# A two-layer graph network on one core: q, k and v by seven half-size products, with x1 parked in DRAM and a new loop order

## The chip, the cores and the metric

The kernel runs on one core of a Trainium2 chip. The metric is the time of one execution in microseconds (us) on the device. The fast runs of each kernel told here lie within 0.36% of each other (3150.13 to 3161.24 us in split_gap, the widest). Each ratio to the kernel before is from runs on one chip. The experiments ran on three chips, on which the kernel before took 2766.76 to 2768.5 us, so times are also compared across them. "Round" means one pass of the kernel's loop: each of its stages works on one of the 128 batches, each stage on another one. SBUF and PSUM are the on-chip memories in which the kernel allocates its tiles; all its matmuls write to PSUM, in tiles of 512 columns, called "banks" here. The "granted clock" is the share of TensorE's full clock that the profile records (1.00 is full speed, 0.50 half).

## The reference, cut to what matters

```
x: (128, 128, 512) float32; adj: (128, 128) float32
# layer 0
h = relu(layernorm(x));  x = x + einsum('nm,bmd->bnd', adj, h) @ W0 + b0         # x1
# layer 1
h = relu(layernorm(x))
q, k, v = split(h @ Wqkv)            # Wqkv 512 x 1536, 8 heads of 64
a = softmax(where(adj == 0, -inf, q k^T / 8))
o = (a v) @ Wp + bp
out = x + o + layernorm(o) * gamma + beta
```

Everything is float32. A product of 512x512 by 512x512 (four batches of 128 rows) stands behind each of q, k and v; Strassen's form does it with seven products of 256x256 by 256x256 in place of eight.

## The kernel before

The parts that the change and the argument touch (cuts marked). Each engine's instructions start in the order in which the program emits them (`manual_schedule`): in this kernel's trace, rounds 7 to 115, TensorE's 8 blocks of a round, VectorE's 23 instructions, ScalarE's 8 and GpSimd's 7 came in that order in 107 of 107 rounds. They wait for each other's results: VectorE for pp, 686.6 us in all. The order of the loop's calls is therefore part of the kernel.

```python
    psum = ctx.enter_context(tc.tile_pool(name="psum", bufs=4, space=bass.MemoryType.PSUM))
    ctx.enter_context(tc.manual_schedule())
    ...
    def stats_of(src):                      # three VectorE steps, then GpSimd
        nc.vector.bn_stats(st, src)
        nc.vector.bn_aggr(mv, st)
        nc.vector.tensor_scalar(ve, mv[:, 1:2], EPS, None, op0=ALU.add)
        nc.gpsimd.tensor_tensor(rs, ve, minus_half, op=ALU.pow)
        return mv[:, 0:1], rs

    def relu_norm(dst, src, mean, rs):      # one VectorE step, then ScalarE
        nc.vector.tensor_scalar(shift, mean, rs, -1.0, op0=ALU.mult, op1=ALU.mult)
        nc.scalar.activation(dst, src, AF.Relu, bias=shift, scale=rs)
    ...
    def qk(i, k):                           # m = 0..7: q and k of a group of four
        for c in range(C):
            nc.tensor.matmul(p, lhsT=wqkv_sb[:, c, m * P:(m + 1) * P],
                             rhs=H1T[g][:, c, :, :].rearrange("p b n -> p (b n)"),
                             start=(c == 0), stop=(c == C - 1))
        nc.scalar.copy(QKT[g][:, m, :, :].rearrange("p b n -> p (b n)"), p)
    ...
    for i in range(2 - LOAD, B + 1):
        at(norm1_out, i + 8)
        ...
        at(scores, i)
        at(softmax_shift, i)
        at(qk, i + G, 0)
        at(flip_probs, i - 1)
        at(softmax_exp, i)
        at(norm0, i + 11)
        at(mix, i + 10)
        at(softmax_divide, i)
        at(norm0_out, i + 11)
        at(qk, i + G, 1)
        at(attend, i - 1)
        at(values, i + 4)
        at(flip, i + 8)
        at(project, i - 1)
        at(finish, i - 1)
        at(layer0, i + 9)
```

What the stages are: `scores` (matmuls ps, VectorE adds the mask), `softmax_shift` (maximum, difference), `softmax_exp` (ScalarE), `softmax_divide` (VectorE sums and reciprocal, GpSimd product sq, then an exchange through DRAM), `flip_probs` (VectorE transpose pT), `attend` (matmuls po, ScalarE copy oT), `project` (matmuls pp, VectorE add o and its statistics), `finish` (VectorE, GpSimd o+x1, VectorE, store). `norm0`, `norm0_out`, `mix` and `layer0` are layer 0; `norm1_out` and `flip` prepare h for q, k and v.

## Time and profile before

| | before |
|---|---|
| time, median of the runs beside the changed kernel | 2768.86 us |
| busy share: TensorE, VectorE, GpSimd, ScalarE | 97%, 59%, 36%, 24% |
| mean granted TensorE clock | 0.987 |
| mean length of a round (batches 7 to 115, from the starts of the oT copy) | 20.70 us |

In the lines below, a timeline row gives start and length in us, the engine, the source line, the operation, what it writes and reads, how many instructions were merged, and in brackets how long the engine had idled before it and what released it. Rows of a merged block end a little after the next block starts, because the ends of matmuls are modelled.

### The profile page before, as it was taken

How to read it: one execution, taken by the hardware profiler on the slowest of the kernel's cores; microseconds unless marked ns; L12 is line 12 of the kernel's file. 1: busy time of each engine (PE TensorE's matmuls, PEld its weight loads, DVE VectorE, ACT ScalarE, POOL GpSimd, SP SyncE). 2: the span in 40 equal slices, each digit the busy share in tenths (PEclk: the TensorE clock that was granted, in tenths of full speed). 3: DMA queues.
4: the chain of work that ended last, by engine and by line, in shares of the span. 5: the costliest groups of instructions: out<-in, count | busy, mean ns of one | idle time of the engine just before them, and what ended most of it. 6: DMA issues, size and time to landing. Idle time of an engine off the chain costs nothing. (4 is left out here: it accounts for less than half of the span.)

```text
span 2762.8 us, 29275 instructions
## 1 busy us (share of the span) xinstructions
PE 2666.9 (97%) x10241; PEld 1312.7 (48%) x10241; DVE 1632.5 (59%) x2951; ACT 666.1 (24%) x1026; POOL 987.8 (36%) x902
## 2 busy tenths in 40 slices
PE   6999999999999999999999999999999999999974
PEld 3444444444444444444444444444444444444432
DVE  3365665665665665665665665665665665665544
ACT  2222222222222222222222222222222222222110
POOL 3233333333333333333333333333333333333222
PEclk9999999999999999999999999999999999999986
DMA  4233333333333333333333333333333333332221
GB/s 165 64 97 105 100 102 104 100 101 104 102 101 103 103 100 103 103 99 103 103 101 103 102 102 102 102 103 100 103 103 103 99 103 104 99 103 96 76 77 61
DMA packets 223636, 276.76 MB, mean 100 GB/s; under 512 B 24704, under 2 KB 155904, under 8 KB 223488
## 3 DMA queue, kind: packets, MB, share of 16 engines
q1 hardware_dynamic: 223488, 274.89, 30.8%
q8 instruction: 80, 1.31, 0.2%
q14 instruction: 68, 0.56, 0.1%
HBM read 140.57 MB, written 134.22 MB: 99 GB/s over the span
## 5 line engine op out<-in xcount | busy, mean ns | idle before, releaser
L194 PE MATMUL pqk<-h1T,wqkv_sb 128*128 128x512 f32 x2048 | 934.5, 600 | 5.7 <-issue 5.7
L127 POOL TENSOR_TENSOR rs<-ve,minus_half 128x1 f32<-128x1 f32 x384 | 266.4, 694 | 1425.8 <-DVE ve L125 1425.8
L142 ACT ACTIVATE h<-x,shift,rs 128x512 f32<-128x512 f32 x256 | 208.3, 814 | 1537.7 <-DVE shift L141 1537.7
L194 PEld LDWEIGHTS pqk<-h1T,wqkv_sb 128*128 128x128 f32 x2048 | 370.3, 190 | 393.8 <-issue 378.8
L263 DVE TENSOR_TENSOR o<-pp,bp_b 128x512 f32<-128x512 f32 x128 | 88.4, 691 | 686.6 <-PE pp L261 686.6
L261 PE MATMUL pp<-wp_sb,oT 128*128 128x512 f32 x1024 | 470.2, 603 | 3.4 <-ACT oT L255 3.4
L203 PE MATMUL pv<-wqkv_sb,h1T 128*128 128x512 f32 x1024 | 473.2, 605 | 0.0
L165 PE MATMUL pl<-w_sb,yT 128*128 128x512 f32 x1024 | 465.5, 598 | 0.0
L261 PEld LDWEIGHTS pp<-wp_sb,oT 128*128 128x128 f32 x1024 | 197.4, 193 | 254.0 <-issue 209.7
L165 PEld LDWEIGHTS pl<-w_sb,yT 128*128 128x128 f32 x1024 | 196.5, 192 | 245.6 <-issue 245.6
L237 POOL TENSOR_TENSOR sq<-s,sm 128x1024 f32<-128x1024 f32 x128 | 244.3, 1908 | 177.9 <-DMA x<-in_x_dram 98.4
L203 PEld LDWEIGHTS pv<-wqkv_sb,h1T 128*128 128x128 f32 x1024 | 184.5, 190 | 207.1 <-issue 207.1
L229 ACT ACTIVATE s<-s 128x1024 f32<-128x1024 f32 x128 | 135.3, 1057 | 364.3 <-DVE s L226 364.3
L273 DVE SCALAR_TENSOR_TENSOR t<-t,rs,o 128x512 f32<-128x512 f32 x128 | 96.2, 751 | 214.1 <-POOL o L272 214.1
L177 POOL TENSOR_TENSOR x<-x,beta_b 128x512 f32<-128x512 f32 x128 | 162.2, 1267 | 152.1 <-ACT h L142 149.3
L252 PE MATMUL po<-pT,v 128*64 128x128 f32 x2048 | 144.5, 285 | 57.0 <-DVE pT L244 50.7
L252 PEld LDWEIGHTS po<-pT,v 128*64 128x64 f32 x2048 | 113.1, 140 | 160.1 <-DVE pT L244 104.1
L121 DVE BATCH_NORM_STATS2 st<-x 128x6 f32<-128x512 f32 x256 | 172.5, 674 | 5.6 <-DMA x<-in_x_dram 1.1
L156 PEld LDWEIGHTS pmix<-adjT,h 128*128 128x128 f32 x1024 | 136.8, 195 | 78.5 <-issue 58.8
L215 PEld LDWEIGHTS ps<-qkT 64*128 64x128 f32 x2048 | 124.2, 187 | 97.1 <-issue 97.1
L151 POOL TENSOR_TENSOR x<-x,b_b 128x512 f32<-128x512 f32 x128 | 161.8, 1264 | 15.0 <-ACT h L142 15.0
L220 DVE TENSOR_TENSOR s<-ps,maskb 128x512 f32<-128x512 f32 x256 | 163.5, 680 | 0.0
(36 smaller groups left out, 2011.1 us busy)
## 6 DMA issues: line engine op xcount, KB each, us to landing
d<-sq SPq DMA_DIRECT2D x128, 512.0 KB, 2.6
sx<-d SPq DMA_DIRECT2D x512, 128.0 KB, 2.9
x<-in_x_dram SPq DMA_DIRECT2D x128, 256.0 KB, 2.7
d<-h SPq DMA_DIRECT2D x128, 256.0 KB, 2.0
h1x<-d SPq DMA_DIRECT2D x512, 64.0 KB, 2.0
out_dram<-t SPq DMA_DIRECT2D x128, 256.0 KB, 2.1
wqkv_sb<-in_L_gnn_w_qkv_dram SPq DMA_DIRECT2D x1, 3072.0 KB, 16.6
w_sb<-in_L_gnn_weight_dram SPq DMA_DIRECT2D x1, 1024.0 KB, 9.2
```

Of the source, the lines that this page charges most:

```text
L121: nc.vector.bn_stats(st, src)
L127: nc.gpsimd.tensor_tensor(rs, ve, minus_half, op=ALU.pow)
L142: nc.scalar.activation(dst, src, AF.Relu, bias=shift, scale=rs)
L151: nc.gpsimd.tensor_tensor(X[i], X[i], b0_b, op=ALU.add)
L165: nc.tensor.matmul(p, lhsT=YT[i][:, c, :], rhs=w0_sb[:, c, :], start=(c == 0), stop=(c == C - 1))
L177: nc.gpsimd.tensor_tensor(X1[i], X1[i], beta_b, op=ALU.add)
L194: nc.tensor.matmul(p, lhsT=wqkv_sb[:, c, m * P:(m + 1) * P], rhs=H1T[g][:, c, :, :].rearrange("p b n -> p (b n)"), start=(c == 0), stop=(c ...
L203: nc.tensor.matmul(p, lhsT=H1T[g][:, c, j, :], rhs=wqkv_sb[:, c, 2 * D:], start=(c == 0), stop=(c == C - 1))
L220: nc.vector.tensor_tensor(s[:, e * C:(e + 1) * C, :], ps[e], m4, op=ALU.add)
L237: nc.gpsimd.tensor_tensor(sq, s.rearrange("p h (q r) -> p q h r", q=Q), sm.unsqueeze(1).unsqueeze(3).to_broadcast([P, Q, H, R]), op=ALU.mult)
L252: nc.tensor.matmul(p[e * HD:(e + 1) * HD, c, :], lhsT=V[i][:, h:h + HD], rhs=PT[i][:, e * C + c, :], start=True, stop=True)
L261: nc.tensor.matmul(p, lhsT=OT[i][:, c, :], rhs=wp_sb[:, c, :], start=(c == 0), stop=(c == C - 1))
```

## The change

The intent is to cut TensorE's work, which fills 97% of the span. For each of q, k and v of a group of four batches, seven products with half the rows, half the columns and half the depth are formed instead of eight. GpSimd forms the four sums of the left factor, VectorE the sums of the weights once at the start. The products are summed partly in the PSUM banks and partly by VectorE adds when a bank is read. To make room in SBUF, x1 is stored in DRAM and loaded again when it is needed; to make room in PSUM, the other matmuls get two banks in place of four. The loop is ordered anew as well.

```diff
-    psum = ctx.enter_context(tc.tile_pool(name="psum", bufs=4, space=bass.MemoryType.PSUM))
+    psum = ctx.enter_context(tc.tile_pool(name="psum", bufs=2, space=bass.MemoryType.PSUM))
 ...
+    def left_factors(g):
 ...
+        nc.gpsimd.tensor_tensor(s1, a21, a22, op=ALU.add)
+        nc.gpsimd.tensor_tensor(s2, s1, a11, op=ALU.subtract)
+        nc.gpsimd.tensor_tensor(s4, a12, s2, op=ALU.subtract)
+        nc.gpsimd.tensor_tensor(s3, a11, a21, op=ALU.subtract)
+        LEFT[g] = (a11, s1, s2, s4, s3, a12, a22)
+    def product(g, kind, k, p):             # four matmuls of 256 columns
 ...
+    def chain(g):                           # 3 x 7 steps, one per "yield"
 ...
+            product(g, kind, 0, X_);  nc.scalar.copy(r1, X_);  yield
+            product(g, kind, 1, Y_);  nc.scalar.copy(r5, Y_);  yield
+            product(g, kind, 2, X_);  nc.scalar.copy(r2, X_);  yield
+            product(g, kind, 3, Y_);  nc.vector.tensor_tensor(c12, Y_, r2, op=ALU.add);  yield
+            product(g, kind, 4, X_);  nc.vector.tensor_tensor(c22, X_, r5, op=ALU.add);  yield
+            product(g, kind, 5, Z_);  nc.vector.tensor_tensor(c11, Z_, r1, op=ALU.add);  yield
+            product(g, kind, 6, X_);  nc.scalar.copy(c21, X_);  yield
 ...
+        X1D[i] = dram.tile([P, D], F32, name="x1d", bufs=14)
+        nc.sync.dma_start(out=X1D[i], in_=X1.pop(i))
 ...   (the loop)
         at(scores, i)
+        at(reload, i - 1)
+        next(step, None)
         at(softmax_shift, i)
-        at(qk, i + G, 0)
+        at(flip, i + 7)
+        at(layer0, i + 8)
+        at(softmax_exp, i)
+        next(step, None)
         at(flip_probs, i - 1)
-        at(softmax_exp, i)
-        at(norm0, i + 11)
-        at(mix, i + 10)
         at(softmax_divide, i)
-        at(norm0_out, i + 11)
-        at(qk, i + G, 1)
+        at(norm1_out, i + 8)
+        at(norm0, i + 10)
+        at(mix, i + 9)
+        next(step, None)
+        at(norm0_out, i + 10)
         at(attend, i - 1)
-        at(values, i + 4)
-        at(flip, i + 8)
+        next(step, None)
+        if j == G - 1 and 0 <= g + 2 < B // G:
+            left_factors(g + 2)
         at(project, i - 1)
         at(finish, i - 1)
-        at(layer0, i + 9)
+        next(step, None)
+        if j == G - 1:
+            next(step, None)
```

(The steps of `chain` are set on one line each here, and their allocations are left out.)

## The prediction

> **What bounds the kernel now.** I read the page's busy shares first, then the timeline of TensorE over a few rounds in the middle, then the timelines of the other engines over the same round.
>
> ```profile
> PE 2666.9 (97%) x10241; PEld 1312.7 (48%) x10241; DVE 1632.5 (59%) x2951; ACT 666.1 (24%) x1026; POOL 987.8 (36%) x902
> ```
>
> TensorE is busy for 97% of the span, no other engine for more than 59%. One round of the loop (one batch in each stage) on TensorE; columns are start us, length us, engine, line, operation, operands, count:
>
> ```profile
> 1403.04 1.05 PE L156 MATMUL pmix<-adjT,h 128*128 128x128 f32 x8
> 1403.93 3.60 PE L194 MATMUL pqk<-h1T,wqkv_sb 128*128 128x512 f32 x8
> ...
> 1408.60 3.70 PE L203 MATMUL pv<-wqkv_sb,h1T 128*128 128x512 f32 x8
> 1412.14 3.60 PE L261 MATMUL pp<-wp_sb,oT 128*128 128x512 f32 x8
> ...
> 1419.10 1.16 PE L215 MATMUL ps<-qkT 64*128 64x128 f32 x16
> ...
> 1423.73 1.05 PE L156 MATMUL pmix<-adjT,h 128*128 128x128 f32 x8
> ```
>
> The round repeats after 20.69 us (1403.04 to 1423.73) and the blocks follow each other with 0.0 to 0.2 us between. pp to pl starts 3.43 us apart (1412.14 to 1415.57 in the same view), so one 512-column instruction, of which there are two per matmul of the program, takes 0.429 us. Eight 128-column ones take 0.89 us, 0.111 each. So TensorE bounds it. But the other engines are in order, and the next three views (same round) show how little slack stands behind that. VectorE:
>
> ```profile
> 1402.58 1.28 DVE L220 TENSOR_TENSOR s<-ps,maskb 128x512 f32<-128x512 f32 x2
> ...
> 1408.42 1.21 DVE L234 TENSOR_REDUCE sm<-s 128x8 f32<-128x1024 f32 x1
> 1409.66 0.20 DVE L235 RECIPROCAL sm<-sm 128x8 f32<-128x8 f32 x1
> 1409.78 0.16 DVE L141 TENSOR_SCALAR shift<-mv,rs 128x1 f32<-128x1 f32 x1
> ...
> 1415.77 0.69 DVE L263 TENSOR_TENSOR o<-pp,bp_b 128x512 f32<-128x512 f32 x1 [5.21 <-PE pp L261]
> ...
> 1419.93 0.75 DVE L273 SCALAR_TENSOR_TENSOR t<-t,rs,o 128x512 f32<-128x512 f32 x1 [1.68 <-POOL o L272]
> ```
>
> GpSimd:
>
> ```profile
> 1403.59 1.27 POOL L177 TENSOR_TENSOR x<-x,beta_b 128x512 f32<-128x512 f32 x1 [1.18 <-ACT h L142]
> 1408.64 0.55 POOL L127 TENSOR_TENSOR rs<-ve,minus_half 128x1 f32<-128x1 f32 x1 [3.79 <-DVE ve L125]
> 1410.10 1.91 POOL L237 TENSOR_TENSOR sq<-s,sm 128x1024 f32<-128x1024 f32 x1 [0.91 <-DMA x<-in_x_dram]
> 1411.96 1.27 POOL L151 TENSOR_TENSOR x<-x,b_b 128x512 f32<-128x512 f32 x1
> ...
> 1418.63 1.26 POOL L272 TENSOR_TENSOR o<-o,x 128x512 f32<-128x512 f32 x1
> ```
>
> ScalarE:
>
> ```profile
> 1409.98 0.81 ACT L142 ACTIVATE h<-x,shift,rs 128x512 f32<-128x512 f32 x1 [1.99 <-DVE shift L141]
> ...
> 1411.16 0.59 ACT L255 COPY oT<-po 128x512 f32<-128x512 f32 x1
> ```
>
> Read them as one ring. VectorE adds the mask (1402.58), takes maximum, difference, sums and reciprocal (to 1409.86), gives ScalarE its shift (1409.78); ScalarE does the relu (1409.98) and then copies oT (1411.16 to 11.75); pp starts at 1412.14; VectorE waits for it (1415.77), finishes the output at 1420.68, adds x1, and begins the next mask at 1423.27. That ring has only tenths of slack: in the waits of this trace the weight load of pp stood for ACT's oT 120 times, 43.3 us in all, 0.36 each. What keeps it short is one detail of POOL: the rs of norm0 (1408.64) is made *before* the 1.91 us sq (1410.10), so the shift finds it ready.
>
> [...]
>
> ```profile
> 37.24 1.16 PE L156 MATMUL pmix<-adjT,h 128*128 128x128 f32 x8 [2.58 <-ACT h L142]
> ...
> 47.05 2.08 PE L156 MATMUL pmix<-adjT,h 128*128 128x128 f32 x8 [5.21 <-ACT h L142]
> ```
>
> After 2.58 us idle eight mix matmuls ran in 1.16 us, after 5.21 us in 2.08, and the pl block that followed took 5.53 instead of 3.60.
>
> **The change on TensorE.** Per group of four batches q, k and v took 48 matmuls = 96 instructions x 0.429 = 41.2 us. Strassen's form has 3 x 7 products x 4 matmuls of 256 columns = 168 instructions x 0.216 = 36.3 us. Weight loads (0.19 us each) stay hidden, since the mix blocks have one every 0.111. Saved: 4.9 us a group, 1.23 us a round, about 158 us in 128 rounds. Against it: 21 blocks a group instead of 12, each waiting for a read of its bank; blocks that wait for another engine now begin 0.1 to 0.2 us late. Estimate 0.3 to 0.6 us a round. TensorE alone would need about 20.0 us a round: 2,670 us in all, 3% less.
>
> **Other work.** ScalarE keeps its 12 copies a group. VectorE gets 9 adds of 128x512 out of PSUM a group (0.69 each as L220 and L263), 1.6 us a round on 12.5: 14 of 20, not full. POOL gets four adds a group, 4 x 1.27 = 5.1 us, 1.3 a round on 7.5. x1's trip is 0.5 MB a round, some 25 GB/s on the page's 100, with the reload a round ahead of its use: hidden. The eight weight sums are some 8 us once.
>
> **The order is what decides.** The diff also moves things in the loop. flip and layer0's add and stats now stand *before* flip_probs on VectorE, inside the ring (they were after the shift, in the idle time, and after the output). And POOL now gets, in this order, sq, x1+beta, rs of norm0; norm0's shift on VectorE waits for that rs, ScalarE's relu for the shift, the oT copy stands behind the relu, project behind oT. Walk the new ring with starts from the trace, each to the start of the next (us):
> - mask adds 1.31, maximum 1.25, difference 1.22, flip 0.70 (its row's mean), x1 add 0.72, stats 0.73 + 0.22 + 0.07, pT 1.17, sums 1.24, reciprocal until sq starts 0.44: 9.07
> - POOL sq 1.86, x1+beta 1.25, rs until the shift 0.58: 3.69
> - shift to relu 0.20, relu to oT copy 0.72, oT to pp 0.98: 1.90
> - pp to o add 3.63, add 0.72, stats 0.73 + 0.22 + 0.23, POOL rs 0.96, o+x1 1.30, last step to the next VectorE work 0.67: 8.46
>
> Sum 23.12 us. By the steps' places in the rounds, five of the nine adds of a group fall inside the ring (the first two steps and the one after finish; the others fall while VectorE waits for POOL or TensorE): 5 x 0.72 / 4 = 0.90. Ring: 24.0 us, against 20.0 for TensorE. **The ring becomes the bound**, and TensorE stands some 4 us before project in each round (its work up to the products before project ends about 11 us after the output, project starts at about 15). By the early trace such a gap is at the edge of costing clock: a throttled project is 1.2 to 2 us longer. I add 0.3 us a round on average: 24.3. POOL's four adds in every fourth round (from about 6.3 to 11.4 us after sq starts) end as project's rs is wanted, so cost about nothing.
>
> **The sum.** The first scores started at 120 us (weight loads begin early; one round later plus 8 us of weight sums, less TensorE work: same). About 120 full rounds: 120 x 24.3 = 2,916. The last nine rounds without layer 0 took 161 us and have the same order: 161. 120 + 2,916 + 161 = 3,197; I say 3,190.
>
> **Rivals.** (1) TensorE stays the bound: 2,600 to 2,680. It needs the ring below 20 us, that is VectorE not waiting for norm0's rs behind sq and beta, or shorter POOL work. The 97% and the clean cadence of before speak for it; the program order read from the diff, and that every engine of before ran in program order, against. Even with only busy times in the ring (no latencies) I get 22 + 0.9 us. (2) The clock falls in every round: project at half speed adds up to 3.4 us, 27 us a round, some 3,550. Gaps of 3.8 us in the early trace were throttled only for a part (mix 1.64 us, pl 4.84), so unlikely as a rule. (3) The queue of SyncE, which now also waits for the x1 store, delays flip or flip_probs: h1x would land some 7 us before its flip, sx more; no effect. (4) PSUM: two mm banks and one of cy and cz. Each bank's reader stands one or two blocks ahead; the waits fall in TensorE's new idle time.
>
> **Range and chances.** The uncertain terms are the clock (0 to 1.2 us a round) and the ring (23.0 to 24.5): 23.0 gives 3,040 and 25.2 gives 3,310. Should I have misread the order, the time falls to rival 1, or to a tie if only part of the ring opens: 6% faster, 4% within 2%, 90% slower.
>
> **What will show it.** Right: a round near 24 us; pp preceded by a TensorE idle of about 4 us released by ACT's oT; VectorE waiting 1.5 to 2.5 us at the shift of norm0 for POOL's rs; rs directly after the x1+beta add; TensorE busy near 80%; instructions of the products 0.216 us apart, 1.73 us a block of eight. Wrong: rounds below 21 us with TensorE above 95% (order misread), or a granted clock below 0.9 (rival 2), or waits at the products' banks or DMAs leading the list of waits.

## The result, and the profile after

| | before | after |
|---|---|---|
| time, median | 2768.86 us | 3312.85 us (3311.79 to 3313.65, 4 runs) |
| TensorE busy | 2666.9 us, 97% | 2774.4 us, 84% |
| mean granted clock | 0.987 | 0.906 |
| mean round | 20.70 us | 25.44 us |

The changed kernel is slower by 19.7%: ratio 1.1968, 95% interval 1.1948 to 1.1989. A ratio here is the mean time of one kernel's fast runs over that of the other's of the same rounds, so it is not quite the ratio of the medians quoted. The results are correct.

The page of the kernel after: busy times, and the row of the granted clock over 40 slices (tenths of full speed):

```profile
PE 2774.4 (84%) x12545; PEld 1829.2 (55%) x12545; DVE 1816.7 (55%) x3247; ACT 675.0 (20%) x1026; POOL 1140.8 (34%) x1030
...
PEclk9999989888989889898998988999988989889997
```

TensorE is no longer at its limit, and its busy time has grown although it does fewer columns: the clock row swings between 8 and 9 for the whole span, where before it stood at 9 until the end.

TensorE's timeline, the blocks around project (pp):

```profile
1621.55 1.99 PE L232 MATMUL cx<-h1T,wqk_sb 128*128 128x256 f32 x8
1627.30 3.70 PE L334 MATMUL pp<-wp_sb,oT 128*128 128x512 f32 x8 [3.75 <-ACT oT L328]
...
1650.00 5.10 PE L334 MATMUL pp<-wp_sb,oT 128*128 128x512 f32 x8 [3.53 <-ACT oT L328]
1654.93 1.89 PE L232 MATMUL cz<-wv_sb,h1T 128*128 128x256 f32 x8
...
1674.79 3.70 PE L334 MATMUL pp<-wp_sb,oT 128*128 128x512 f32 x8 [2.49 <-ACT oT L328]
```

In each round pp stands after an idle gap that ScalarE's oT copy ends: 2.5 to 4.0 us, 3.4 on average over rounds 7 to 115. The block at 1627.30 takes 3.5 us (the next one starts at 1630.84). The one at 1650.00 takes 4.9 us (to 1654.93), for the same eight instructions.

VectorE, GpSimd and ScalarE in the round before 1627.30:

```profile
1612.13 1.28 DVE L292 TENSOR_TENSOR s<-ps,maskb 128x512 f32<-128x512 f32 x2
...
1621.61 0.20 DVE L307 RECIPROCAL sm<-sm 128x8 f32<-128x8 f32 x1
...
1625.71 0.21 DVE L155 TENSOR_SCALAR shift<-mv,rs 128x1 f32<-128x1 f32 x1 [2.22 <-POOL rs L141]
1631.04 0.69 DVE L336 TENSOR_TENSOR o<-pp,bp_b 128x512 f32<-128x512 f32 x1 [5.11 <-PE pp L334]
```

```profile
1622.04 1.91 POOL L309 TENSOR_TENSOR sq<-s,sm 128x1024 f32<-128x1024 f32 x1 [2.63 <-DVE shift L155]
1623.91 1.26 POOL L191 TENSOR_TENSOR x<-x,beta_b 128x512 f32<-128x512 f32 x1
1625.13 0.55 POOL L141 TENSOR_TENSOR rs<-ve,minus_half 128x1 f32<-128x1 f32 x1
```

```profile
1625.96 0.81 ACT L156 ACTIVATE h<-x,shift,rs 128x512 f32<-128x512 f32 x1 [2.75 <-DVE shift L155]
1626.68 0.56 ACT L328 COPY oT<-po 128x512 f32<-128x512 f32 x1
```

This is the ring as the prediction read it from the diff. The reciprocal ends at 1621.81, sq follows on GpSimd, then x1+beta, then rs of norm0 (1625.13 to 1625.68); VectorE, idle for 2.22 us, makes the shift at 1625.71; ScalarE does relu and oT; pp starts at 1627.30; VectorE takes its output at 1631.04. From the view of waits:

```profile
PE pp L334 <- ACT oT L328: 400.4, 122, 4.0
...
DVE shift L155 <- POOL rs L141: 313.9, 135, 3.1
```

VectorE's wait for rs was 111.6 us in all before and is 313.9 now. TensorE's own wait for oT was 3.4 us before and is 400.4.

The same kernel in stretches of 1 us around the pp block at 1650.00 (after the busy times of TensorE, weight loads, VectorE, ScalarE and GpSimd come the granted clock, the DMA share and GB/s):

```profile
1648.00:1649.00 1.00, 0.00 (x0) 0.00 (x0) 0.58 (x2) 0.34 (x1) 0.38 (x1) 1.00 0.77 307
1649.00:1650.00 1.00, 0.00 (x0) 0.00 (x0) 0.23 (x1) 0.95 (x2) 0.44 (x1) 0.72 0.00 0
1650.00:1651.00 1.00, 1.00 (x1) 0.50 (x2) 0.00 (x0) 0.00 (x0) 1.00 (x2) 0.50 0.45 125
1651.00:1652.00 1.00, 1.00 (x3) 0.47 (x2) 0.00 (x0) 0.00 (x0) 1.00 (x1) 0.50 0.98 278
1652.00:1653.00 1.00, 1.00 (x3) 0.46 (x2) 0.00 (x0) 0.00 (x0) 0.92 (x2) 0.58 0.91 251
1653.00:1654.00 1.00, 1.00 (x3) 0.38 (x2) 0.00 (x0) 0.00 (x0) 0.92 (x2) 1.00 0.38 130
```

The clock halves some 3 us after TensorE went idle (at about 1646.5), stays at 0.50 for about 3.4 us and comes back at about 1652.8. Project, the block that ends the gap, has a granted clock of 0.50 for its first 2.8 us.

### The profile page after: what moved, and what is told of

The parts are those of the page before. It is cut to its first block, busy times and chain, and to the rows that moved or that the text cites. A ratio compares the mean times of both kernels' runs of the same rounds, so it can differ in the third digit from the quotient of the medians.

```text
span 3311.1 us, 34928 instructions
## 1 busy us (share of the span) xinstructions
PE 2774.4 (84%) x12545; PEld 1829.2 (55%) x12545; DVE 1816.7 (55%) x3247; ACT 675.0 (20%) x1026; POOL 1140.8 (34%) x1030
## 5 line engine op out<-in xcount | busy, mean ns | idle before, releaser
L334 PE MATMUL pp<-wp_sb,oT 128*128 128x512 f32 x1024 | 717.4, 866 | 400.4 <-ACT oT L328 400.4
L334 PEld LDWEIGHTS pp<-wp_sb,oT 128*128 128x128 f32 x1024 | 275.5, 282 | 779.6 <-ACT oT L328 449.4
L232 PE MATMUL cy<-sum,wqk_sb 128*128 128x256 f32 x1024 | 251.8, 389 | 2.4 <-POOL sum L214 2.4
L232 PE MATMUL cx<-h1T,wqk_sb 128*128 128x256 f32 x1024 | 250.1, 388 | 0.9 <-DVE qkT L269 0.9
L232 PE MATMUL cx<-sum,wqk_sb 128*128 128x256 f32 x1024 | 243.7, 381 | 6.5 <-issue 6.5
L232 PEld LDWEIGHTS cx<-sum,wqk_sb 128*128 128x128 f32 x1024 | 193.4, 191 | 72.2 <-issue 52.0
L155 DVE TENSOR_SCALAR shift<-mv,rs 128x1 f32<-128x1 f32 x256 | 48.5, 190 | 314.0 <-POOL rs L141 313.9
L232 PEld LDWEIGHTS cy<-sum,wqk_sb 128*128 128x128 f32 x1024 | 186.9, 190 | 52.0 <-issue 25.0
L232 PEld LDWEIGHTS cx<-h1T,wqk_sb 128*128 128x128 f32 x1024 | 188.2, 191 | 45.3 <-issue 13.0
```

The lines of the kernel that those rows point to most:

```text
L232: nc.tensor.matmul(p[:, half, :], lhsT=lhsT, rhs=rhs, start=first and half == 0 and c == 0, stop=k in (3, 5, 6) and c == 1, skip_group_che ...
L334: nc.tensor.matmul(p, lhsT=OT[i][:, c, :], rhs=wp_sb[:, c, :], start=(c == 0), stop=(c == C - 1))
```

## Experiments

Ten kernels were run, all correct, all in three timed rounds beside the kernel before. The **ring theory** says that the new order closed a loop of dependences longer than TensorE's work. The **clock theory** adds that TensorE's idle gap in each round lowers its clock. The rivals are that the products themselves cost TensorE more than their columns, that project is slow because of its bank or weights, and that x1's trip to DRAM delays something.

"Slow pp" below is a pp block longer than 4 us, counted over up to about 110 rounds in the middle of the profiled run (some rounds fall on a border of the views and are not counted). The time from oT's start to VectorE's add of o contains pp; it is 4.35 to 4.40 us with an undisturbed clock in all variants of the changed kernel whose project was not moved, so what is above 4.37 on average is put down to the clock.

| kernel | time us | ratio to before | mean round us | clock part of it us | slow pp |
|---|---|---|---|---|---|
| before | 2768.86 | 1 | 20.70 | 0 | 0 |
| after | 3312.85 | 1.197 | 25.44 | 2.0 | 85 of 93 |
| split_gap | 3156.53 | 1.140 | 23.84 | 0.4 | 24 of 99 |
| beta_late | 3033.97 | 1.096 | 23.04 | 0.8 | 53 of 103 |
| rs_first | 3033.28 | 1.096 | 23.04 | 0.9 | 56 of 103 |
| keep_busy | 3105.11 | 1.123 | 23.45 | 0 | 0 of 101 |
| order_alone | 3247.48 | 1.174 | 24.75 | 1.5 | 48 of 96 |
| order_alone_deep | 3144.52 | 1.136 | 23.89 | 1.2 | 68 of 100 |
| products_old_order | 2880.08 | 1.041 | 21.61 | 0 | 0 of 110 |
| x1_dram_alone | 2768.69 | 1.000 | 20.70 | 0 | not counted |
| open_ring_plain | 2732.24 | 0.988 | 20.57 | not in the ring | not counted |
| open_ring | 2572.36 | 0.929 | 19.34 | not in the ring | not counted |

### keep_busy: more work for TensorE in the gap

```diff
     def project(i):
         p = mm_psum("pp")
+        for c in range(3):
+            nc.tensor.matmul(p, lhsT=wp_sb[:, c, :P], rhs=wp_sb[:, c, :], start=True, stop=True)
         for c in range(C):
```

> The changed kernel with six extra matmul instructions (three calls of 128x512, 2.6 us) put into TensorE's idle time right before project, into project's own bank, which project then overwrites. Ring theory with the clock: TensorE gets 330 us more work and the kernel is faster, because the idle gap falls from 3.7 to about 1 us, project takes 3.4 us, the ring stays at 23.4: 3,050 to 3,090 us. Rival (project is slow because of its bank or its weights, or TensorE's amount of work sets the time): 3,310 or more.

Measured: 3105.11 us, 208 us less than the changed kernel and 15 us above what was expected, though TensorE does 128 times 2.6 us more. TensorE's timeline, the added block and project:

```profile
1622.58 2.74 PE L334 MATMUL pp<-wp_sb 128*128 128x512 f32 x6
1626.29 3.70 PE L336 MATMUL pp<-wp_sb,oT 128*128 128x512 f32 x8 [0.98 <-ACT oT L328]
1629.83 1.89 PE L232 MATMUL cz<-wv_sb,h1T 128*128 128x256 f32 x8
```

The gap before pp is 1.0 us here, and pp takes 3.5 us (1626.29 to 1629.83) in every round; the mean clock is 0.990. The bank and the weights of pp are as before, so they were not what made it slow. This bears out the clock theory: the clock lost to the idle gap costs 2.0 us a round (25.44 less 23.45), beside the waiting itself. It also gives the ring alone: 23.45 us a round. (From the 120th round to the end it took some 20 us longer than the changed kernel, 173 us against 154; the expectation was missed there.)

### split_gap: the same idle time in two pieces

```diff
-        next(step, None)
         at(norm0_out, i + 10)
         at(attend, i - 1)
         next(step, None)
+        next(step, None)
```

> The changed kernel with attend moved one product block earlier (norm0_out and attend now before the third product step). No work and no step of the ring changes; TensorE's idle time of 3.7 us in one piece before project falls into two pieces, about 2.4 us before attend and 2 us before project. Clock theory (the loss above my prediction is project at a lowered clock after the idle gap, 2.0 us a round): project takes 3.4 us again, rounds 23.4 to 23.7 us, 3,060 to 3,120 us in all. Rival (project is slow for another reason, its bank or its weights): 3,310 us, project still 5 to 6 us.

Measured: 3156.53 us, 156 us less than the changed kernel, but 37 us above the range expected. TensorE's timeline, a round:

```profile
1626.54 1.09 PE L325 MATMUL po<-pT,v 128*64 128x128 f32 x16 [2.47 <-DVE pT L316]
...
1633.31 3.70 PE L334 MATMUL pp<-wp_sb,oT 128*128 128x512 f32 x8 [2.03 <-ACT oT L328]
```

The gaps are 2.47 us before attend's po and 2.03 us before pp, as expected, and the ring is the same 23.4 us (23.84 less the clock's 0.4). The clock still fell in 24 of 99 rounds: 2 us of idling was not yet safe. That was not expected; the reason is under beta_late.

### beta_late: one GpSimd step out of the ring

```diff
-        nc.gpsimd.tensor_tensor(X1[i], X1[i], beta_b, op=ALU.add)      # in norm1_out, with the store
+    def add_beta(i):  (the same add and the store)
 ...
         at(norm1_out, i + 8)
         at(norm0, i + 10)
+        at(add_beta, i + 8)
```

> The changed kernel with x1+beta moved behind norm0's rs on GpSimd; nothing else. Ring theory: 1.25 us leave the ring, the round falls by that and the idle gap to about 2.5 us: 3,160 us if the clock still falls in most rounds, 2,930 if it no longer does. Rival (the time is TensorE's own, from the products): 3,310, no change, as GpSimd is busy for only 34%.

Measured: 3033.97 us, between the two values. Moving 1.25 us of GpSimd work, an engine that is busy for 34%, took 279 us off. From the start of finish's last VectorE step to the next oT copy the ring fell by 1.22 us (14.90 to 13.68), and the clock part fell from 2.0 to 0.8 us. Three pp blocks:

```profile
1603.10 5.40 PE L336 MATMUL pp<-wp_sb,oT 128*128 128x512 f32 x8 [2.33 <-ACT oT L330]
...
1626.97 3.70 PE L336 MATMUL pp<-wp_sb,oT 128*128 128x512 f32 x8 [1.28 <-ACT oT L330]
...
1649.54 3.70 PE L336 MATMUL pp<-wp_sb,oT 128*128 128x512 f32 x8 [2.53 <-ACT oT L330]
```

After 2.33 us of idling pp ran slow (5.40), after 2.53 us it ran at full speed. The traces' record of the granted clock shows what differs. In each of the twelve traces the clock changes only on a grid of 3.413 us that runs through the whole execution (no change lies more than 1 ns off it). The stretches of that grid around the first and the last of these blocks (length, then busy times of TensorE, weight loads, VectorE, ScalarE and GpSimd, granted clock, DMA share and GB/s):

```profile
1600.66:1604.07 3.41, 1.08 (x4) 0.49 (x4) 0.81 (x2) 1.28 (x2) 3.41 (x5) 1.00 0.38 154
1604.07:1607.48 3.41, 3.41 (x6) 1.35 (x5) 0.00 (x0) 0.00 (x0) 3.25 (x3) 0.50 0.43 131
...
1645.03:1648.44 3.41, 1.98 (x10) 1.42 (x8) 1.43 (x7) 2.01 (x4) 2.94 (x3) 1.00 0.06 25
1648.44:1651.86 3.42, 2.32 (x6) 1.13 (x7) 0.00 (x0) 1.53 (x3) 1.93 (x2) 1.00 0.46 172
1651.86:1655.27 3.41, 3.41 (x18) 2.21 (x18) 1.89 (x5) 0.21 (x1) 0.03 (x1) 1.00 0.66 187
```

The gap of 2.33 us (1600.77 to 1603.10) lies in one stretch; TensorE was busy for 1.08 us of it, 32%, and the next stretch ran at half clock. The longer gap of 2.53 us (1647.01 to 1649.54) is cut by a border at 1648.44; TensorE was busy for 58% and 68% of the two stretches, and the clock held. Rounds 7 to 115 of all twelve traces agree. After each of the 252 full-speed stretches in which TensorE was busy for less than 41%, the clock halved; after the 7,637 with 46% or more it never did; in between, it halved after 155 of 186. In the changed kernel's trace alone it halved after 101 of 101, 0 of 551 and 0 of 3.

### rs_first: norm0 before softmax_divide, as before the change

```diff
+        at(norm0, i + 10)
         at(softmax_divide, i)
         at(norm1_out, i + 8)
-        at(norm0, i + 10)
```

> The changed kernel with norm0 (its statistics and rs) emitted before softmax_divide, one line moved: rs stands before sq and x1+beta on GpSimd, as in the kernel before. Ring theory: 3.7 us of GpSimd leave the ring, 1.1 us of VectorE statistics and some 1.5 us of ScalarE (relu of norm1, two copies before relu of norm0) take part of the place: rounds near 22.3 us, 2,950 us if the clock holds, 3,150 if not. Rival (TensorE's own time): 3,310.

Measured: 3033.28 us, 23.04 us a round, of which 0.9 us is the clock; so the ring is 22.1 us, near the 22.3 us expected. Taking the whole of GpSimd's 3.7 us out gave only 1.3 us. As I read it, ScalarE's relu of norm1 and two copies stand before relu of norm0 and become the next link: in a round of the trace these four steps and oT fill ScalarE without a gap from 1620.02 to 1622.98 us, from just after the reciprocal to the start of pp (1623.03).

### order_alone and order_alone_deep: the order without the products

The kernel before, with its ordinary q, k and v, its four banks and x1 in SBUF, got the changed kernel's order of the loop:

```diff
         at(scores, i)
+        at(qk, i + G, 0)                 # order_alone has it after softmax_exp
         at(softmax_shift, i)
+        at(flip, i + 8)                  # order_alone: all of these one batch less ahead
+        at(layer0, i + 9)
+        at(softmax_exp, i)
         at(flip_probs, i - 1)
         at(softmax_divide, i)
+        at(norm1_out, i + 9)
+        at(norm0, i + 11)
+        at(mix, i + 10)
 ...
```

> The kernel before (ordinary q, k and v, x1 kept in SBUF, four mm banks) with the loop order of the changed kernel: flip and layer0 before flip_probs, norm1_out and norm0 behind softmax_divide. Ring theory: the ring of the changed kernel less the product adds, 23.4 - 0.9 = 22.6 us against TensorE's 20.7: 2,980 us, up to 3,050 with some clock loss. Rival (the products or the fewer banks made it slow): 2,770, as before.

> As order_alone, but flip, layer0, norm1_out, mix, norm0 and load one batch further ahead, so that q and k no longer wait in one of four rounds for the flip of the same round (that wait, 4.6 us, was of my own making there). Ring theory: every round as the undisturbed ones of order_alone, 22.7 us at full clock, TensorE 20.7, an idle gap of 1.9 us before project that lowers the clock in about half of the rounds by 1.7 us: 22.7 to 23.6 us a round, 3,000 to 3,110 us. Rival (the products or fewer banks are needed for the loss): 2,770.

Measured: order_alone 3247.48 us, well above what was expected; in one round of four q and k waited for the flip of the same round, up to 4.6 us, which I had built in. Its other rounds had 22.71 us at full clock. order_alone_deep, without that fault: 3144.52 us, 35 us above its range, with 22.71 us in rounds of full clock and the clock lost in 68 of 100. Two of its pp blocks:

```profile
1641.28 5.40 PE L261 MATMUL pp<-wp_sb,oT 128*128 128x512 f32 x8 [1.88 <-ACT oT L255]
...
1665.69 3.70 PE L261 MATMUL pp<-wp_sb,oT 128*128 128x512 f32 x8 [1.89 <-ACT oT L255]
```

The same gap of 1.9 us, once with a slow and once with a full-speed pp: the first lies whole in one stretch of the clock's grid (1638.19 to 1641.60), the second is cut by a border at 1665.49. So the order alone makes the kernel of before 13.6% slower, with not one product or bank changed: the rival that the products are needed for the loss is out.

### products_old_order: the products without the new order

```diff
+        at(norm1_out, i + 7)
         at(load, i + LOAD)
         at(scores, i)
         at(reload, i - 1)
         at(softmax_shift, i)
+        next(step, None)
         at(flip_probs, i - 1)
         at(softmax_exp, i)
+        at(norm0, i + 10)
+        at(mix, i + 9)
         at(softmax_divide, i)
         at(norm0_out, i + 10)
 ...   (steps after norm0_out and attend, then flip, project, finish, a step, layer0, a step)
```

> The changed kernel's products, sums, banks and x1 in DRAM, in the loop order of the kernel before (one step shallower). Ring theory: the ring of before, near 20.4, plus six product adds of a group that fall in it, 1.05: some 21.3 us a round, TensorE at 19.4 below it: 2,790 to 2,880 us, no gain from fewer matmul columns. Rival (products bound TensorE, order doesn't matter): 3,200 or more. Rival 2 (products gain at once in the good order): 2,610.

Measured: 2880.08 us, 4.1% slower than before, at the upper end of the range. Two pp blocks:

```profile
1614.57 3.70 PE L334 MATMUL pp<-wp_sb,oT 128*128 128x512 f32 x8 [1.21 <-ACT oT L328]
...
1636.23 3.70 PE L334 MATMUL pp<-wp_sb,oT 128*128 128x512 f32 x8 [1.21 <-ACT oT L328]
```

The gap is 1.2 us, the clock holds, and TensorE still waits for oT. So in the old order too something other than TensorE's work sets the round, and fewer columns gain nothing. That it is the ring, with product adds in it, is what was expected; no run here takes the adds out alone.

### x1_dram_alone: only the trip to DRAM

```diff
         nc.gpsimd.tensor_tensor(X1[i], X1[i], beta_b, op=ALU.add)
+        X1D[i] = dram.tile([P, D], F32, name="x1d", bufs=14)
+        nc.sync.dma_start(out=X1D[i], in_=X1.pop(i))
 ...
         at(scores, i)
+        at(reload, i - 1)
```

> The kernel before with x1 stored to DRAM after its beta and loaded again a round ahead of its use; nothing else. Hidden transfers: 2,760 to 2,780 us, 20.7 us a round. Rival (the store, in SyncE's queue between the two exchanges, delays the flips or slows the other transfers): 2,820 or more.

Measured: ratio 1.0002, interval 0.9987 to 1.0017. The trip is hidden.

### open_ring and open_ring_plain: the ring opened

VectorE's part of project is put off to the next round, behind softmax_shift, so that no engine waits within a round for project. norm0's rs comes before sq, attend before softmax_divide, norm1_out at the top. open_ring_plain has the same order with ordinary q, k and v.

```diff
+        at(norm1_out, i + 7)
         at(scores, i)
+        at(reload, i - 2)
         next(step, None)
         at(softmax_shift, i)
+        at(project_out, i - 2)           # VectorE: o = pp + bp, its statistics
+        at(flip_probs, i - 1)
+        at(softmax_exp, i)
+        at(layer0, i + 8)
         next(step, None)
+        at(norm0, i + 10)
         at(mix, i + 9)
         next(step, None)
         at(attend, i - 1)
+        at(finish, i - 2)                # first VectorE step and o + x1
         next(step, None)
+        at(softmax_divide, i)
+        at(norm0_out, i + 10)
+        at(flip, i + 7)
+        at(finish_out, i - 2)            # last VectorE step and the store
 ...
         at(project, i - 1)               # the matmuls alone
         next(step, None)
```

> The seven products in another order of the loop: the VectorE part of project and finish is done one round later, norm1_out at the top, attend before softmax_divide, norm0's rs before sq. Project's output is no longer waited for within the ring. Ring theory: TensorE becomes the bound again at 20.0 to 20.3 us a round, no idle gap above 1 us, 2,640 to 2,700 us, faster than both kernels. Rival (the products themselves cost more than their columns): 2,800 or more, with TensorE busy over 95%.

> The kernel before with the order of open_ring (project's VectorE part a round later and so on), ordinary q, k and v. If open_ring's gain is the seven products': TensorE bounds as before, 20.7 us a round, 2,740 to 2,780 us. If the gain is the order's alone: near 2,570.

Measured: open_ring 2572.36 us, 7.1% faster than before (ratio 0.9292, interval 0.9278 to 0.9306) and faster than its expectation; open_ring_plain 2732.24 us, 1.2% less than before (a difference under 2%, which counts as the same), just below its expectation. The page of open_ring, busy times, and the chain that ended last:

```profile
PE 2496.5 (97%) x12545; PEld 1750.0 (68%) x12545; DVE 1987.3 (77%) x3247; ACT 706.1 (27%) x1026; POOL 1209.8 (47%) x1030
...
PE 95%; DVE 3%; DMA 1%; issue 1%; ACT 0%; POOL 0%; SPq 0%; POOLq 0%; DVEq 0%; ACTq 0%
```

TensorE is at its limit again and makes 95% of the chain. Project follows the product before it and is followed by the next without a gap:

```profile
1418.97 3.60 PE L336 MATMUL pp<-wp_sb,oT 128*128 128x512 f32 x8
1422.40 1.89 PE L234 MATMUL cz<-wv_sb,h1T 128*128 128x256 f32 x8
...
1439.60 3.60 PE L336 MATMUL pp<-wp_sb,oT 128*128 128x512 f32 x8
```

Between the mean rounds of open_ring_plain and open_ring, 20.57 and 19.34 us, lie 1.23 us: just what the prediction worked out for the products' columns (4.9 us a group). The products, with the banks and the x1 trip that go with them, were worth 6%, once nothing else held the round. The 0.3 to 0.6 us a round that I had charged for the start of more blocks did not show up, which is why open_ring came out below its expectation: TensorE needs 19.3 us a round, not 20.0.

## Why the prediction was wrong, point by point

**The direction and the mechanism held.** TensorE's saving is real (1.23 us a round between open_ring_plain and open_ring; the 0.216 us taken for an instruction of 256 columns was an estimate, and eight of them took 1.73 us in the trace after, 1654.93 to 1656.66) and was not to be had in the new order, because the ring sets the round. order_alone_deep shows that the order does it; rs directly behind sq and x1+beta, VectorE's wait at norm0's shift (2.2 us in the round shown, 2.8 in another) and pp's wait for oT are in the trace as the prediction listed them. x1's trip is hidden (x1_dram_alone, ratio 1.0002); the banks and GpSimd's four sums show in no wait of TensorE of weight (2.4 us in all for the sums, 0.9 us for the add that reads cx). That VectorE keeps its order shows in the changed kernel: one product's block ended at 935.04 us, but its add started only at 937.12, behind norm0's shift, which waited 2.19 us for rs.

**The ring was sized a little too long.** Predicted 24.0 us; measured 23.45 us (keep_busy, whose rounds have no clock part; the changed kernel's own segments give 14.90 + 4.16 + 4.37 = 23.43). I took 0.98 us from oT's start to pp's from the kernel before, where pp also waited for the block ahead of it; it is 0.62 us here (1626.68 to 1627.30).

**The step that failed is the term for the clock.** "I add 0.3 us a round on average" should have been 2.0 us: 6.39 us from oT's start to the add of o on average, against 4.37 at full clock. Over 120 rounds that is some 200 us more than allowed; the shorter ring gives back 65. The difference, 139 us, lies near the 123 us between 3,190 and 3,313. I had taken a gap of about 4 us as "at the edge of costing clock", leaning on the start of the trace before alone, where the blocks after a single gap of 2.58 us took 1.16 (mix) and 3.60 us (pl), after one of 3.82 us 1.64 and 4.84, against 1.05 and 3.60 in the middle of the trace. What counts, by the runs, is how much idling falls into one stretch of the clock's grid: all 252 full-speed stretches with less than 41% of work, over 2.0 us of idling in 3.41 us, were followed by one at half clock, none of the 7,637 with 46% or more, up to 1.84 us of idling. A gap of 3.5 us nearly always leaves one such stretch (80 of 82 pp blocks after gaps of 3.5 us and more ran slow), and pp, which ends the gap, runs in the next. With half-speed clock from one stretch pp took 4.9 to 5.2 us instead of 3.5 (52 blocks), from two 6.1 to 6.6 (50 blocks; rounds 7 to 115 of the changed kernel); averaged over all rounds the clock cost 2.0. The range's upper end took at most 1.2 us for the clock and missed by 3 us. It also did not add its own two terms: the ring at 24.5 with 1.2 us of clock is 25.7 us a round, not 25.2, which by the prediction's sum gives some 3,365 us in place of 3,310.

**Where the 4.7 us a round come from,** by the runs: the order 2.0 us (22.71 at full clock in order_alone_deep, against 20.70), the products with all that goes with them 0.7 us (23.45 against 22.71; that these are the product adds in the ring, for which the prediction had 0.9, is argued, not shown), the clock 2.0 us (25.44 against 23.45).

**Rival 2 of the prediction** (the clock falls in every round) came closer than I gave it credit for: it fell in 85 of 93 rounds, but for part of project only.

## What to carry to other kernels

Before taking work off the busiest engine, add up the ring of in-order waits that runs beside it: in this kernel it was within tenths of TensorE's round, and a reordering that looked neutral, with GpSimd at a third of its time, made it nearly 3 us longer than that. Put the reading of a late result (here project's output) a round later, so that no engine waits for it in the same round; then the saved columns count in full. And count TensorE's idle time in stretches of 3.4 us: in the rounds counted here the clock never fell where at least 46% of each stretch was work, and no gap of up to 1.7 us before project cost it (none of 316), while each of 252 stretches with less than 41% cost half the clock for at least the next 3.4 us. Here filler matmuls in the gap made the changed kernel 6% faster.

## What else the traces show

- Project after gaps of different length, over rounds 7 to 115 of the changed kernel, split_gap, beta_late, rs_first, keep_busy, products_old_order and both order_alone kernels: slow blocks were none of 316 after gaps up to 1.7 us, 180 of 308 after 1.9 to 2.2 us, 110 of 166 after 2.3 to 2.8 us, 80 of 82 after 3.5 us and more.
- A float32 matmul of the program shows up as two instructions, each with its own weight load (12545 of each on the page of the changed kernel). An instruction of 512 columns took 429 ns, one of 256 columns 216 ns. The loads are 0.19 us long in the trace, but the mix blocks have one every 0.11 us, so even there they hide.
- In open_ring finish's last VectorE step and GpSimd's work overlap (VectorE's and GpSimd's timelines):

```profile
1399.52 0.74 DVE L350 SCALAR_TENSOR_TENSOR t<-o,mv,gamma_b 128x512 f32<-128x512 f32 x1
...
1421.85 1.97 DVE L356 SCALAR_TENSOR_TENSOR t<-t,rs,o 128x512 f32<-128x512 f32 x1
```

```profile
1421.36 1.91 POOL L311 TENSOR_TENSOR sq<-s,sm 128x1024 f32<-128x1024 f32 x1 [1.02 <-issue]
1423.23 1.72 POOL L167 TENSOR_TENSOR x<-x,b_b 128x512 f32<-128x512 f32 x1
```

  The step took 1.97 us beside sq (1.99 on average over 128), where the same kind of step took 0.74 us in the same kernel and 0.75 us before; the GpSimd add after sq took 1.72 us in place of 1.26 before. The step shown ended at 1423.82, 0.55 us after sq. Why the two steps are longer there no run here shows. TensorE was the bound, busy for 97%, so this did not set the round.
